# A fused four-layer image kernel: tables made during sampling, the channel norm run backwards with the rows' way back behind it, the columns' way back beside the rows' way ahead, and the next pair's loads issued after the quarter-size convolution

## The chip, the cores and the metric

The kernel runs on one core of a Trainium2 chip, in float32. The metric is the device time of one execution in microseconds (us); lower is better. Five engines work side by side, each through its own instructions in order: PE (matrix products; its weight loads are listed as PEld), DVE (vectors), ACT (activations), POOL (general), and SP, which here only issues DMAs. ACT and POOL can issue DMAs too.

## The reference

The input x has 8 images of 64 channels and 128 x 128 pixels. Four layers follow one another, each adding to x what it makes of a group norm of x (`_gn`, 32 groups of 2 channels):

```python
x = x + L0(_gn(x))   # deformable 3x3 convolution, batch norm over all 8 images, relu
x = x + L1(_gn(x))   # plain 3x3 convolution, 64 to 64 channels
x = x + L2(_gn(x))   # state-space scan along rows and along columns
x = x + L3(_gn(x))   # convolution with stride 4, neighbours, 3x3 convolution, resize by 4
```

L0 makes 18 offsets and 9 masks per pixel with convolutions, samples the image bilinearly at the 9 displaced places and multiplies with the weights. Its batch norm takes mean and variance over all images, so nothing of L1 can start before L0 has ended for every image. L2 does this twice, with the pixels in row order (direction 0) and in column order (direction 1):

```python
fx = layer_norm(seq)                 # over the 64 channels of a pixel
Bu = einsum(fx, B_bar)               # drives 64 complex states
xf = scan(Bu); xb = reversed scan(Bu)
h  = 2 * real(concat(xf, xb) @ C) + D * fx
y  = gelu(h) + fx
y  = layer_norm(y) @ enc.T @ dec.T + layer_norm(y)
```

and fuses both results with a 1x1 convolution. L3 reduces the image to 32 x 32 pixels with a 4 x 4 convolution of stride 4, finds for each pixel the nine least similar ones within a 7 x 7 window, averages their difference, convolves, gates each channel, and enlarges by 4.

## The kernel before

Images are worked on in pairs: partition = image of the pair x channel, so there are four pairs p = 0 to 3. `deform()` does L0 for all pairs, then `rest()` does L1 to L3 pair by pair. The order of the calls in the Python code is the order of priority; a scheduler places each engine's instructions from it with a model of their durations, and an instruction waits by semaphores for its data, for a free buffer of its tag (`bufs`) and, where a pool takes over the addresses of a closed one, for the last reader of those addresses.

**Sampling** (`deform`). Per pair a table of pixels with their neighbours is written to DRAM (`fill`), after `statistics` for the group norm. For 512 pixels at a time, `sample` issues on POOL one indirect DMA for each tap, image and 128 pixels (L379: 9216 in all), DVE multiplies by weights (L388) and sums four corners (L389), PE transposes (L393, L395) and multiplies (L402). A function `work()` is called after every nine gathers, 256 times in a pair; it advances `near` (the offsets of the next 1024 pixels) each time, and `far` (statistics and table of the next pair, 42 steps) every fifth time.

**The setup** (`setup_rest`) follows sampling: the batch norm's scale and bias from `ystat` (L480 to L488), then `setup_scan` (a long chain of small DVE instructions that makes the state tables `tabs` and the output tables `outs` of both directions and stores them in DRAM, L808 and L809), then `setup_nearest` (scales of L3, the mask `window`, the block-diagonal `wa`).

**Per pair.** Two SBUF tiles of the size of an image, `room0` and `room1`, take turns.

- `finish_deform`: x comes in by eight DMAs on SP (L501) and the sampled y by eight on ACT's queue (L503) into a tile with three buffers; ACT applies the batch norm and relu (L504), POOL adds (L505), DVE takes statistics (L507), and `groupnorm` ends it.
- `conv3x3`: L1, PE (L560) and DVE (L562, L566); between its steps it advances `aside`, which is `neighbours` (most of L3) of the pair before.
- `first_norm`: the centred image and its variance per pixel (PE L859 and L824, ACT L861 and L862), then the scale 1/sigma, spread over the channels by POOL (L830) and PE (L833), multiplied in by DVE (L851). It goes through the image in eight steps of 16 rows, n = 0 to 7.
- `scan_direction`, for rows and then for columns, in 16 groups of 1024 pixels. The **way back** goes from the last group to the first: `inputs` (ACT L900, four DMAs on SP L902) puts the pixels in scan order, `drive` (PE L911 and L914, ACT L913, DVE L918, POOL L919) makes the drive u, `scan` (PE L930, ACT L931, DVE L933) the states z, and z is stored to DRAM (L949). The **way ahead** goes from the first group to the last, with `inputs`, `drive` and `scan` again, `rebuilt` (reads z of the way back, L958; PE L962, POOL L966 and L968, DVE L967), `outputs` (PE L981, ACT L983, DVE L984), `deviation` (PE L993 and L997, ACT L995) and `add` (PE L833 and L1012, DVE L1013 and L1017). Before this change the rows' way back starts when `first_norm` has ended, and the columns' way back when the rows' way ahead has.
- `finish_deform` of the next pair, then `down` of this one: its weights `l_wd` (L160, L162), the bias (L1093), scaled weights (L1097), 32 products in two sums (L1103), relu (L1104), store of the small image `kept` (L1107) and of the image to `y` (L1108).

PSUM, where PE writes, has eight banks here: tags "x", "b" and "y" with two buffers each, "small" and "bs" with one. The way back takes "b" and "y" in turn for `drive`; the way ahead takes "b" for `drive` and `rebuilt`.

Of the kernel before, what the change touches and what calls it, by code (L numbers as in the profile page):

```python
# [9 lines left out]
F32 = mybir.dt.float32  # L10
# [6 lines left out]
P = 128  # L17
C = 64
# [22 lines left out]
class Net:  # L41


    def __init__(self, tc, ctx, ins, out):
# [9 lines left out]
        self.ystat = self.const.tile([P, self.npair * NCH, 6], F32, name="ystat")  # L54
# [110 lines left out]


    def deform(self):
# [6 lines left out]
        with ExitStack() as ctx:  # L174
# [242 lines left out]
            for p in range(self.npair):  # L417
                more = p + 1 < self.npair
                far = chain(statistics(p + 1), fill(p + 1)) if more else iter(())
                for e in range(NCH // 2):  # L420
# [6 lines left out]
                    def work(near=near, far=far, count=count):  # L427
                        count[0] += 1
                        next(near, None)
                        if count[0] % 5 == 0:  # L430
                            next(far, None)
# [8 lines left out]
    def rest(self):  # L440
        tc = self.tc
        with ExitStack() as ctx:
            pool = lambda name, bufs, **kw: ctx.enter_context(tc.tile_pool(name=name, bufs=bufs, **kw))
            self.big = pool("b_big", 1)
            self.keep = pool("b_keep", 1)
# [6 lines left out]
            self.state_tab = [self.dram.tile([P, NSTATE], F32, name=f"state_tab{d}") for d in range(2)]  # L452
            self.out_tab = [self.dram.tile([P, NOUT], F32, name=f"out_tab{d}") for d in range(2)]
            self.setup_rest()
# [5 lines left out]
            for p in range(self.npair):  # L460
# [4 lines left out]
                if p + 1 < self.npair:  # L465
                    other = tile_(p + 1, f"room{(p + 1) % 2}")
                    r, nb = self.finish_deform(p + 1, image(other))
                aside = self.neighbours(p, self.down(p, a, r3, nb3))
# [4 lines left out]
    def setup_rest(self):  # L473
        tc, nc, ins, keep = self.tc, self.nc, self.ins, self.keep
        psum = self.ps1

        gamma = self.vec(keep, "gamma", ins["gamma"])
# [12 lines left out]
        self.setup_scan()  # L490
        self.setup_nearest()
# [101 lines left out]
    def setup_scan(self):  # L593
# [12 lines left out]
        with tc.tile_pool(name="b_scan_setup", bufs=1) as sp:  # L606
            pp = self.ps
# [17 lines left out]
            nc.vector.tensor_scalar(phase, phase, -math.pi, math.pi, ALU.max, ALU.min)  # L625
            sin, cos = tl("sin"), tl("cos")
# [65 lines left out]

            for d in range(2):
# [13 lines left out]
                while n < NB:  # L707
# [5 lines left out]
                    n *= 2  # L713

# [13 lines left out]
                for name, gu, gv in (("b", gre, sgim), ("bs", gim, sgre)):  # L728
# [3 lines left out]
                    bm.append(m)  # L732

                mats = tabs[:, MAT : MAT + T * P].rearrange("p (f a q) -> p f a q", f=2, a=2)
                for k in range(T):
# [3 lines left out]
                    tp = pp.tile([P, P], F32, tag="x", name=f"tp{k}_{d}")  # L739
                    nc.tensor.transpose(tp, m, eye)  # L740
                    for f, j in ((0, T - 1 - k), (1, k)):
                        half = slice(j % 2 * C, j % 2 * C + C)
                        nc.vector.tensor_copy(mats[half, f, j // 2], tp[half])

# [22 lines left out]
                for name in ("ln1_g", "ln1_b", "D"):  # L767
                    s[name] = self.vec(keep, f"{name}{d}", ins[name][d])

                for k in range(1 - T, T):  # L770
                    c_ = om[:, 0, k - 1] if k > 0 else om[:, 1, T + k] if k else both_c
                    gp = pp.tile([P, C], F32, tag="x", name=f"gp{k}_{d}")
# [499 lines left out]
```

## Time and profile before

| | us |
|---|---|
| median of 3 runs | 17387.34 (17378.91 to 17398.45) |
| profiled execution, its own time | 17399.76 |
| its span, first to last instruction | 17398.0 |
| mean granted PE clock | 0.826 |

From the trace, where the stages lie (us from the start of the span; pair 2 stands for all):

| stage | from | to |
|---|---|---|
| sampling, all pairs | 224.9 (first gather) | 11951.8 |
| setup | 11951.8 | 12030.5 (first load of x) |
| `finish_deform`, pair 0 | 12030.5 | 12097.7 |
| pair 2: `first_norm` | 14918.6 | 15003.6 |
| pair 2: rows, way back | 15003.6 | 15092.7 |
| pair 2: rows, way ahead (L981) | 15090.1 | 15399.7 |
| pair 2: columns, way back (L949) | 15413.8 | 15493.9 |
| pair 2: columns, way ahead (L981) | 15491.3 | 15802.1 |
| `finish_deform` of pair 3 | 15823.9 | 15893 |
| `down` of pair 2 | 15893 | 15954 |

One execution's trace gives these; a stage is read from the first and last instruction of the lines named. A row of the stage view gives, for a stretch of time, the busy time of each engine in it and its number of instructions, the granted PE clock (1 is full), the share of time in which the 16 DMA engines were busy, and GB/s. Products in float32 are recorded as two PE instructions each. Matmuls are pipelined, so that their busy time is not a measure of PE at its peak.

### The profile page before, as it was taken

What the parts mean: (1) busy time and instruction counts of PE and PEld (TensorE: products, weight loads), DVE (VectorE), ACT (ScalarE), POOL (GpSimd) and SP (SyncE); (2) the same over time, 40 slices, a digit from 0 to 9 for tenths busy, and PEclk for the clock granted to TensorE, in tenths of its full rate; (3) what the DMA queues carried; (4) which work ended last, traced back from release to release, by engine and by line L of the source; (5) the groups of instructions that cost most, each with busy time, mean ns of one, the idle gap of its engine ahead of it and who ended that gap; (6) DMA issues with size and microseconds to landing.
All of it is one profiled execution on the core that took longest, in us unless ns stands there. A gap on an engine that the chain in (4) does not pass through costs nothing. (4 is left out here: it accounts for less than half of the span.)

```text
span 17398.0 us, 124024 instructions
## 1 busy us (share of the span) xinstructions
PE 11757.7 (68%) x33912; PEld 4169.8 (24%) x33912; DVE 11724.9 (67%) x27470; ACT 2920.7 (17%) x4957; POOL 10355.3 (60%) x10489
## 2 busy tenths in 40 slices
PE   5666656656666655666666566533887887887887
PEld 1111111111111111111111111111443443443443
DVE  5777777777777777777777777775564565565565
ACT  1111111011111111111110100001331332332331
POOL 3777777777777777777777777774231232232231
PEclk8877778778877877788878778766998898998998
DMA  6444444444444444444433333333122222222222
GB/s 199 130 138 134 132 136 126 126 129 131 138 134 132 120 131 128 137 135 132 129 116 114 117 114 114 112 107 118 50 64 91 86 64 94 85 65 93 86 63 73
DMA packets 965241, 1968.72 MB, mean 113 GB/s; under 512 B 215740, under 2 KB 516548, under 8 KB 930756
## 3 DMA queue, kind: packets, MB, share of 16 engines
q0 software_dynamic: 442368, 1208.55, 23.7%
q1 hardware_dynamic: 513332, 714.84, 13.4%
q10 hardware_dynamic: 8848, 37.40, 0.6%
q8 instruction: 275, 4.51, 0.1%
q14 instruction: 418, 3.42, 0.1%
HBM read 1515.79 MB, written 276.47 MB: 103 GB/s over the span
## 5 line engine op out<-in xcount | busy, mean ns | idle before, releaser
L379 POOL DMA_INDIRECT g<-table,idx x9216 | 8908.4, 967 | 2811.8 <-issue 2598.9
L388 DVE TENSOR_TENSOR g<-g,wts 128x256 f32<-128x256 f32 x9216 | 3807.8, 419 | 3147.4 <-DMA g<-table,idx 3125.5
L389 DVE TENSOR_REDUCE sm<-g 128x64 f32<-128x256 f32 x9216 | 4978.4, 579 | 0.5
L313 PE MATMUL po<-xe,wt 128*54 128x512 f32 (+3 forms) x8384 | 4780.2, 681 | 54.7 <-ACT ob L323 52.8
L393 PE MATMUL sp<-ident,sm 128*128 128x128 f32 x4096 | 1526.6, 377 | 4108.8 <-DVE sm L389 4099.2
L393 PEld LDWEIGHTS sp<-ident,sm 128*128 128x128 f32 x4096 | 628.4, 155 | 6927.5 <-DVE sm L389 4985.3
L396 ACT COPY s<-sp 128x512 f32<-128x512 f32 x1024 | 600.0, 586 | 8571.9 <-PE sp L393 8571.6
L313 PEld LDWEIGHTS po<-xe,wt 128*54 128x54 f32 x8384 | 931.4, 140 | 1440.4 <-issue 1078.0
L919 POOL TENSOR_TENSOR u<-u,vs 128x512 f32<-128x512 f32 x256 | 347.2, 1356 | 1174.7 <-DVE vs L918 1096.7
L402 PE MATMUL yp<-s,wd 128*64 128x512 f32 (+1 forms) x2560 | 816.1, 654 | 14.3 <-ACT s L396 14.3
L560 PE MATMUL c<-room,l_w 128*64 128x508 f32 (+1 forms) x3072 | 721.5, 597 | 16.7 <-DMA room<-nx 9.2
L900 ACT ACTIVATE fx<-room,ln_b,ln_g 128x512 f32<-128x512 f32 x512 | 646.6, 1292 | 145.9 <-DMA in<-fx 77.5
L911 PE MATMUL pv<-in,tabs 128*128 128x512 f32 x1024 | 560.5, 655 | 61.2 <-DMA in<-fx 58.2
L830 POOL COPY l_yb<-ln_y 128x512 f32<-128x512 f32 x128 | 78.8, 615 | 871.1 <-PE l1v L824 662.5
L395 PE MATMUL s<-ident,sm 128*64 128x128 f32 x1024 | 348.4, 340 | 334.2 <-DVE sm L389 297.2
L981 PE MATMUL py<-in,outs 128*128 128x512 f32 x1024 | 519.0, 611 | 0.0
L981 PE MATMUL py<-x,outs 128*128 128x512 f32 x1024 | 484.1, 594 | 0.0
L933 DVE TENSOR_TENSOR_SCAN z<-tabs,z,u 128x256 f32<-128x256 f32 x512 | 388.8, 778 | 100.6 <-POOL u L919 93.8
L968 POOL TENSOR_TENSOR x<-x,xt 128x512 f32<-128x512 f32 x256 | 324.8, 1269 | 201.8 <-DVE xt L967 201.8
L984 DVE TENSOR_TENSOR h<-h,in 128x512 f32<-128x512 f32 x256 | 285.7, 1118 | 229.8 <-ACT h L983 225.6
L1017 DVE SCALAR_TENSOR_TENSOR room<-room,bias,rs 128x256 f32<-128x256 f32 x512 | 391.4, 823 | 8.9
L397 ACT COPY s<-s 64x128 f32<-64x128 f32 x1024 | 264.1, 258 | 678.1 <-PE s L395 677.7
(1432 smaller groups left out, 10737.0 us busy)
## 6 DMA issues: line engine op xcount, KB each, us to landing
g<-table,idx POOLq DMA_INDIRECT x9216, 2.8
table<-q SPq DMA_DIRECT2D x512, 256.0 KB
in<-fx SPq DMA_DIRECT2D x1024, 128.0 KB
xe<-in_x_dram SPq DMA_DIRECT2D x56, 1408.0 KB
xs<-in_x_dram SPq DMA_DIRECT2D x32, 1024.0 KB
xt<-in_x_dram SPq DMA_DIRECT2D x32, 1024.0 KB
y<-ys SPq DMA_DIRECT2D x128, 256.0 KB
room<-in_x_dram SPq DMA_DIRECT2D x32, 1024.0 KB
```

Source lines behind the costliest of these rows:

```text
L313: nc.tensor.matmul(po[:, r0:r1, c0:c1], lhsT=wt[:, t, :], rhs=xe[:, row + r0 : row + r1, c0 + dx : c1 + dx], start=n == 0, stop=n == len(u ...
L379: nc.gpsimd.indirect_dma_start(out=tq[:, k, :], out_offset=None, in_=flat[i], in_offset=bass.IndirectOffsetOnAxis(ap=idx[:, at : at + 1], ...
L388: nc.vector.tensor_mul(t[:, k], t[:, k], w)
L389: nc.vector.tensor_reduce(sm[:, k], t[:, k].rearrange("p q c -> p c q"), axis=mybir.AxisListType.X, op=ALU.add)
L393: nc.tensor.transpose(sp[:, j, :], sm[:, j * P : (j + 1) * P], self.ident)
L396: nc.scalar.copy(st[i][:, 0:4, m * P : (m + 1) * P], sp)
L402: nc.tensor.matmul(yp[i * C : (i + 1) * C, :], lhsT=wd[0:rows, j, :], rhs=st[i][0:rows, j, :], start=j == 0, stop=j == 4)
L560: nc.tensor.matmul(o, lhsT=lt, rhs=mv, start=k < 2, stop=k >= len(calls) - 2)
L900: nc.scalar.activation(fx[:, e].rearrange("p h (o m) -> p h o m", m=inner), src[:, e::2], AF.Identity, bias=w["ln1_b"], scale=w["ln1_g"])
L911: nc.tensor.matmul(pv, lhsT=tabs[:, at : at + P], rhs=fx[:, :, h, :], start=h == 0, stop=h == 1)
L981: nc.tensor.matmul(py, lhsT=lt, rhs=mv, start=n == 0, stop=n == len(calls) - 1)
L1017: nc.vector.scalar_tensor_tensor(at, at, w["bias"], rs[:, j], ALU.add, ALU.add)
```

## The change

1. **Tables in sampling.** `setup_scan` and `setup_nearest` become generators, 36 steps in all, and are put ahead of `far` of pair 0; they use the PSUM tag "s1" of sampling. `far` is advanced at every third call of `work()` instead of every fifth, in all pairs. Only the batch norm's scale and bias stay after sampling (`setup_deform`). `window` goes to DRAM and is loaded again in `neighbours` of each pair; `wa` is loaded there too.
2. **Norm from the last rows.** `first_norm` runs n = 7 to 0 and yields after each scaled step; after every yield the rows' way back is advanced twice. It takes the tags of the scan's pool for its temporary tiles.
3. **Columns' way back beside rows' way ahead.** `ahead` of direction 0 advances `back` of direction 1 once per group. `drive` uses the PSUM tag "b" everywhere. The tag "in" has two buffers instead of three; the columns' way back has tags of its own with one buffer ("inb", "zbk") and shares "fx", "v" and "u". In `ahead`, `inputs` and `drive` of group g + 2 come ahead of `deviation` of group g.
4. **Loads beside the quarter-size convolution.** `finish_deform` of the next pair is called at the end of `down`, inside its pool, instead of ahead of it.

```diff
+    def run(self):
+        with tc.tile_pool(name="keep", bufs=1) as self.keep:
+            with tc.tile_pool(name="ystat", bufs=1) as sp:
+                self.ystat = sp.tile([P, self.npair * NCH, 6], F32, name="ystat")
+                self.deform()
+                with tc.tile_pool(name="bn0_ps", bufs=1, space=PSUM) as psum:
+                    self.setup_deform(psum)
+            self.rest()
...
                 far = chain(statistics(p + 1), fill(p + 1)) if more else iter(())
+                if p == 0:
+                    far = chain(self.setup(ps_s1, "s1"), far)
...
-                        if count[0] % 5 == 0:
+                        if count[0] % 3 == 0:
                             next(far, None)
...
-            self.setup_rest()
...
-                if p + 1 < self.npair:
-                    other = tile_(p + 1, f"room{(p + 1) % 2}")
-                    r, nb = self.finish_deform(p + 1, image(other))
-                aside = self.neighbours(p, self.down(p, a, r3, nb3))
+                other = tile_(p + 1, f"room{(p + 1) % 2}") if p + 1 < self.npair else None
+                kept, norm = self.down(p, a, r3, nb3, image(other) if other is not None else None)
+                if norm:
+                    r, nb = norm
+                aside = self.neighbours(p, kept)
...
-        for n in range(NCH // 4):
+        for n in range(NCH // 4 - 1, -1, -1):
...
             if late:
                 scale(*late)
+                yield
             late = n, self.rsqrt(self.small, pv, 32, EPS, "ln32")
         scale(*late)
+        yield
...
+            ways = [Scan(self, wp, p, d, a, b, st) for d in range(2)]
+            back = ways[0].back("in", "z", "h")
+            for _ in self.first_norm(wp, p, a, b, r, nb):
+                next(back)
+                next(back)
+            for _ in back:
+                pass
+            ways[0].ahead(ways[1].back("inb", "zbk", "fx"))
+            ways[1].ahead(iter(()))
...
-            out = wp.tile([P, 2, 2, NB], F32, tag="in", name=f"in{p}_{d}{f}_{g}", bufs=3)
+        out = wp.tile([P, 2, 2, NB], F32, tag=itag, name=f"in{name}", bufs=1 if itag == "inb" else 2)
...
+    def back(self, itag, ztag, stage):
+        order = range(NG - 1, -1, -1)
+        fx, u, z = None, None, None
+        for n in range(-2, NG):
+            made = self.drive(1, order[n + 1], fx) if 0 <= n + 1 < NG else None
+            if n + 2 < NG:
+                fx = self.inputs(1, order[n + 2], itag, stage)
+            if n >= 0:
+                z = self.scan(1, order[n], u, z, ztag)
+                self.nc.sync.dma_start(self.net.back[self.d][order[n]], z[:, :, 0:NB])
+            u = made
+            yield
...
+    def ahead(self, aside):
+        self.outs = self.wp.tile([P, NOUT], F32, tag="outs", name=f"outs{self.p}_{self.d}", bufs=1)
+        self.nc.sync.dma_start(self.outs, self.net.out_tab[self.d])
+        fxs, us, xs, late, z = {}, {}, None, None, None
+        for g in range(-2, NG + 1):
+            if 0 <= g + 1 < NG:
+                z = self.scan(0, g + 1, us.pop(g + 1), z, "z")
+            hs = self.outputs(g, fxs.pop(g), xs) if 0 <= g < NG else None
+            if 0 <= g + 1 < NG:
+                xs = self.rebuilt(g + 1, z)
+            if late:
+                self.add(*late)
+            if g + 2 < NG:
+                fxs[g + 2] = self.inputs(0, g + 2, "in", "fx")
+                us[g + 2] = self.drive(0, g + 2, fxs[g + 2])
+            late = (g, hs, self.deviation(g, hs)) if 0 <= g < NG else None
+            next(aside, None)
+        for _ in aside:
+            pass
...
             for n in range(4):
                 s = slice(n * 4096, (n + 1) * 4096)
                 nc.sync.dma_start(self.y[p][:, s], af[:, s])
-        return kept
+            return kept, (self.finish_deform(p + 1, nxt) if nxt is not None else None)
...
+                self.window = wp.tile([P, self.BAND], F32, name=f"window{p}", bufs=1)
+                nc.sync.dma_start(self.window, self.window_tab)
...
+                wa = self.block_diag(sp, f"wa{p}", ins["wa"].rearrange("a (t b) -> a t b", t=1), 1, C)[:, 0, :]
```

## The prediction

> **What bounds the kernel now.** I read the page's 40 slices first, to find its regimes, then the groups of instructions for the longest of them.
>
> ```profile
> PE   5666656656666655666666566533887887887887
> DVE  5777777777777777777777777775564565565565
> POOL 3777777777777777777777777774231232232231
> ...
> L379 POOL DMA_INDIRECT g<-table,idx x9216 | 8908.4, 967 | 2811.8 <-issue 2598.9
> ```
>
> Two regimes: sampling for 27 slices, then four pairs. In sampling the gathers L379 follow one another with 0.30 us between them for which the profile names no other engine ("issue"): 313 start in 400 us while a table is filled (1.278 us each) and 318 where none is (1.258 us). POOL's own issue bounds sampling; DVE has a fifth of its time free. Then the stage view, with stretches cut at the first and last instruction of each stage. Its columns are length, busy time of PE, PEld, DVE, ACT and POOL (instructions in brackets), granted PE clock, DMA share, GB/s.
>
> ```profile
> 11951.70:12030.00 78.30, 18.93 (x56) 13.34 (x56) 64.09 (x383) 2.17 (x4) 2.49 (x12) 0.53 0.15 39
> ```
>
> ```profile
> 14918.00:15003.00 85.00, 77.47 (x450) 55.87 (x450) 42.33 (x155) 40.53 (x64) 19.69 (x32) 0.90 0.00 1
> 15003.00:15093.00 90.00, 60.29 (x137) 24.80 (x138) 46.34 (x69) 56.41 (x68) 22.02 (x16) 0.88 0.57 151
> 15093.00:15384.00 291.00, 265.25 (x1013) 133.31 (x1013) 185.18 (x412) 98.28 (x147) 120.31 (x105) 1.00 0.18 44
> 15384.00:15494.00 110.00, 87.31 (x265) 39.32 (x264) 63.95 (x120) 55.40 (x76) 30.25 (x24) 0.91 0.47 125
> 15494.00:15825.00 331.00, 293.14 (x1141) 147.53 (x1139) 229.99 (x496) 98.46 (x154) 125.28 (x112) 0.98 0.22 65
> 15825.00:15893.00 68.00, 6.32 (x27) 6.01 (x27) 29.72 (x76) 16.75 (x8) 37.62 (x9) 0.50 0.65 251
> 15893.00:15954.00 61.00, 60.77 (x78) 16.83 (x78) 0.22 (x1) 0.97 (x2) 0.17 (x1) 0.93 0.00 0
> ```
>
> The first row is the setup: DVE alone, one small instruction after another. The others are pair 2: norm, rows back, rows ahead, columns back (with edges of its neighbours), columns ahead, the next pair's `finish_deform` (PE empty, DMA at 251 GB/s) and `down` (PE alone). The last two share nothing. Norm and ways ahead, though, are already PE stages, so what is put beside them adds PE work. How much is in the timeline of a way ahead:
>
> ```profile
> 15200.50 0.19 PEld L981 LDWEIGHTS py<-x,outs 128*128 128x128 f32 x1 [0.24 <-issue]
> 15200.93 0.19 PEld L981 LDWEIGHTS py<-x,outs 128*128 128x128 f32 x1 [0.24 <-issue]
> 15201.36 0.19 PEld L981 LDWEIGHTS py<-x,outs 128*128 128x128 f32 x1 [0.24 <-issue]
> ...
> 15204.46 1.08 PE L1012 MATMUL pm<-h,outs 128*64 128x256 f32 x8
> 15207.27 0.66 PE L833 MATMUL 2_0_4_1_rb<-ident,2_0_4_1_yb 128*128 128x128 f32 x4 [1.72 <-POOL 2_0_4_1_yb L830]
> 15207.76 1.02 PE L911 MATMUL pv<-in,tabs 128*128 128x512 f32 x2
> ```
>
> One pass of 512 columns is issued every 0.43 us, and in a group of 20.0 us (POOL's L830 at 15200.59 and 15220.59) PE has one real gap, 1.72 us.
>
> **What the Trainium skill says.** "Perfetto Trace Analysis", section Optimization Strategy, advises interleaving regimes whose most-contended engine differs. The rows above agree for `finish_deform` and `down`, and for setup and sampling; they don't for the ways, where PE leads on both sides. "TensorE: Matmul & The Clock Gate", section Why this matters for your kernels, wants no PE gaps over about 3 us, or the clock drops: clock 0.50 in `finish_deform`, 0.88 on the way back, 1.00 on the way ahead agree. "SBUF — State Buffer", section Who interferes with whom, has DVE copies and tensor-scalar operations in a two-port mode lock GpSimd out; no row here isolates that, so it only bounds a cost below.
>
> **Part 1, tables in sampling.** Removed from the path: 11951.8 to 12030.5. Left is the batch norm's scale and bias, ready at 11962.5 (L488). Relu L504 started at 12045.5, 9.7 us after the first load of y was issued; issued at about 11954 that load lands at 11964, so the pair starts 81 us earlier. I take 78 (65 if addresses come free later, 82 at most). Added to sampling: at most the stage's 383 DVE instructions, 64.1 us, beside 2900 us of pair 0's sampling of which DVE has a fifth free; 12 POOL instructions, 2.5 us, which do hold up gathers; 56 PE passes and a change of ACT's table, both engines waiting there anyway; many small DMAs on SP, where they stand between table stores, not gathers. If each DVE instruction locked POOL out, 64 us; if none, 2.5. I take 8. `far` at every third call does the same fills in 126 calls instead of 210: the 0.020 us that a gather loses to a fill is paid on the same number of stores, so 0 (-40 to +40). Reloading `window` and `wa` is three DMAs a pair under `conv3x3`; only the last pair could show it: 1 us (0 to 4).
>
> **Part 2, norm and rows back.** Now 171.5 us from the first L859 (14918.6) to the rows' first L981 (15090.1). PE busy time is 77.5 + 60.3 = 138. The way back's issue is less: four pv and two pt passes at 0.43 and 0.36 for pn are 2.94 us a group, 47 in sixteen, making 125. DVE (88) and ACT (97) fit below. Not shared are the start (about 8 us until a first step is scaled and read) and the end: after the last scaled step the way back has three steps left at 90/16 = 5.6 us, with PE half idle. I take 155, a gain of 16 a pair (0 if the chains run in series, 35 at PE's sum), 64 in all.
>
> **Part 3, columns back beside rows ahead.** Now 401.2 us from the rows' first L981 (15090.1) to the columns' (15491.3): 15.5 groups of 20.0 us and 91.6 after the last L981 (15399.7). The columns' way ahead still has to wait for the single `outs` buffer, freed by the last L1012 at 15422.3; with a load of some 4 us the 91.6 become 30. So 61.6 us go, and each of 15.5 groups gets x longer: 2.94 us of new PE work less what falls into the gap of 1.72, so at least 1.2. I take x = 2.9, nothing filled, because new chains bring new waits: six uses a group of the two "b" banks instead of four, three "in" buffers become two, one "fx" for two users, and u of the way back must wait for its scan. That is 61.6 - 45 = 16 a pair, 64 in all. Behind a PE instruction that waits for "b" stand L981 and L993, and behind them gelu and DVE. Ends: x = 1.2 gains 43 a pair, x = 5.6 (a whole step of the way back in series) loses 25.
>
> **Part 4, loads beside `down`.** `down` waited for addresses: its memset of `l_wd` came at 13242.8 in pair 0, right behind the last L505, although its norm was ready at 13191.8. Inside the pool it needs none of `finish_deform`'s: weights at about 13192, L1097 till 13197, 58 us of L1103, relu at 13256. `finish_deform` takes its 68 us from 13184 as before, to about 13252, being bound by DMA and POOL, which `down` doesn't use. What is late next is `down`. `conv3x3`, now first active at 13317.7, starts at about 13260: 57 us, three times, 171 (45 to 62 each). Moved queue positions: the loads L501 on SP now follow `kept` (L1107), which waits for the relu, and L503 on ACT follows L1104. But the scheduler already put the stores L1108 at 13184.4 ahead of `kept`, so it doesn't keep call order on SP.
>
> **Sum.** 78 - 8 - 1 + 64 + 64 + 171 = 368 us. The span falls from 17398.0 to 17030; the profiled run has 1.8 us around its span and lay 12.4 above the median, so a median of about 17020.
>
> **Rivals.**
> (a) *Better packing*: waits fall into PE's idle time, x = 1.2 and norm plus rows back 136 us. For it: PE idles 9% of the way ahead, a third of the way back.[...] 78 - 9 + 140 + 172 + 171 = 552, median 16836.
> (b) *PSUM jam*: x = 5.6, and nothing from part 2. For it: "b" alone, where the way back had "b" and "y". Against: each use holds a bank some 3 us of 23. 78 - 9 + 0 - 100 + 171 = 140, median 17248.
> (c) *The loads don't come beside `down`*: L501 or L503 stays queued behind the relu, or addresses still clash. 368 - 171 = 197, median 17190.
> (d) *Sampling slows*: denser fills and DVE's small instructions lengthen gathers. For it: the 0.020 us that a fill costs now, and the port lock. It decides from 368/9216 = 0.040 us a gather; at 0.060 it costs 553, so 17398 - 368 + 553 = 17583 of span, median 17573, 186 slower. Against: gathers never waited for DVE longer than their own issue gap.
>
> **How the numbers follow.** 0.2%, 35 us, is about what a measurement tells from no change. Chances: forecast 0.56, (a) 0.15, (b) 0.12, (c) 0.08, (d) 0.09, of which 0.02 ends within 35 us of before and 0.07 above. So faster 0.91, same 0.02, slower 0.07. The range, 16860 to 17220, takes in the forecast's ends and (c), half of (a) and half of (b).
>
> **What would show it.** In the new profile: no setup stage and a first L501 near 11955; gathers still 313 to 318 in 400 us; `down` and `finish_deform` under each other, 60 us less from the end of a way ahead to L546; rows ahead at about 23 us a group with PE without its gap; 155 us from the norm's first product to L981. A group at 25 us or a gather at 1.31 us would make the forecast wrong.

## Result and profile after

The changed kernel takes 17284.35 us (median of 5 runs, 17278.66 to 17314.63) against 17387.34 us (5 runs): a ratio of 0.9941, 95% interval 0.9925 to 0.9956. That is 103 us less, where 368 were forecast. The profiled execution spans 17276.9 us against 17398.0, 121.1 less.

Cut at the same instructions in both traces, the difference lies here (us, all four pairs together):

| stage | before | after | difference |
|---|---|---|---|
| start to the first activation of `conv3x3` (L546, now L557) | 12097.7 | 12066.6 | -31.1 |
| `conv3x3`, from there to the norm's first product (L859, now L879) | 1007.1 | 1000.4 | -6.7 |
| norm and rows' way back, to the rows' first L981 (now L1208) | 703.1 | 749.6 | +46.5 |
| rows' way ahead, to the columns' first L1208 | 1594.9 | 1592.8 | -2.1 |
| columns' way ahead, `down` and `finish_deform`, to the next L557 (last pair: to its first L975) | 1744.7 | 1619.3 | -125.4 |
| from there to the end | 250.5 | 248.2 | -2.3 |

Parts 1 and 4 paid, less than forecast; part 2 cost time; part 3 did nothing. In the third row one of the four pairs of before is unlike the others: 188.8 us at a granted clock of 0.78, where the other three take 171.3 to 171.6 at 0.88 and 0.89. Against those three the changed kernel's 186.7 to 187.7 us are a loss of some 16 us a pair, more than the sum shows. The 40 slices and the gathers' group of the page after:

```profile
PE   5766565656676656666565665642898898898897
POOL 3777777777777777777777777776132132232231
...
L388 POOL DMA_INDIRECT g<-table,idx x9216 | 8942.7, 970 | 2813.3 <-issue 2617.2
```

The two regimes are still there, and POOL's own issue still bounds sampling (2617.2 us of idle time put to "issue", 2598.9 before). The slices of the pairs have fuller PE digits, and that alone looks like success. The stage view says otherwise. These rows are: what is left between the last gather and the first load of x; pair 2's norm with rows' way back; rows' way ahead; the wait ahead of `down`; `down`.

```profile
11987.50:12001.90 14.40, 7.54 (x20) 2.03 (x20) 6.65 (x7) 1.43 (x3) 0.00 (x0) 0.74 0.20 68
14811.40:14999.00 187.60, 153.59 (x579) 93.70 (x579) 88.22 (x215) 93.06 (x131) 38.73 (x48) 0.79 0.27 69
14999.00:15304.00 305.00, 281.88 (x990) 134.08 (x989) 203.55 (x408) 126.64 (x181) 124.59 (x106) 0.99 0.28 71
...
15732.00:15757.00 25.00, 8.55 (x37) 8.32 (x38) 11.58 (x34) 4.19 (x2) 10.78 (x3) 0.51 1.01 374
15757.00:15822.70 65.70, 58.64 (x71) 14.61 (x71) 19.58 (x47) 14.13 (x9) 29.29 (x10) 0.94 0.38 144
```

The row of the setup has gone. The second row is the surprise. Cut at the same products, the stage before has this row:

```profile
14918.60:15090.10 171.50, 134.43 (x579) 79.00 (x580) 86.11 (x216) 96.16 (x131) 41.11 (x48) 0.89 0.30 79
```

Then 579 PE instructions took 134.4 us; now 579 take 153.6 us, at a granted clock of 0.79 instead of 0.89. Nothing was added and PE got busier: the same products run more slowly. Why, the experiments on part 2 show. The fourth row is what is left unhidden of the loads: 25 us in which the DMA engines are full and PE has little to do.

### The profile page after: what moved, and what is told of

The parts are those of the page before. It is cut to its first block, busy times and chain, and to the rows that moved or that the text cites. A ratio compares the mean times of both kernels' runs of the same rounds, so it can differ in the third digit from the quotient of the medians.

```text
span 17276.9 us, 123578 instructions
## 1 busy us (share of the span) xinstructions
PE 11831.8 (68%) x33912; PEld 4204.3 (24%) x33912; DVE 11804.3 (68%) x27470; ACT 2924.7 (17%) x4956; POOL 10377.4 (60%) x10492
## 3 DMA queue, kind: packets, MB, share of 16 engines
q1 hardware_dynamic: 514532, 715.93, 13.5%
## 5 line engine op out<-in xcount | busy, mean ns | idle before, releaser
L388 POOL DMA_INDIRECT g<-table,idx x9216 | 8942.7, 970 | 2813.3 <-issue 2617.2
L849 POOL COPY l_yb<-ln_y 128x512 f32<-128x512 f32 x128 | 76.6, 615 | 1025.2 <-PE l1v L843 665.9
L1208 PE MATMUL py<-in,outs 128*128 128x512 f32 x1024 | 531.0, 622 | 1.8 <-ACT h L1210 1.8
L1208 PE MATMUL py<-x,outs 128*128 128x512 f32 x1024 | 506.0, 607 | 5.1 <-POOL x L1193 4.9
L1192 DVE TENSOR_TENSOR xt<-zt,tabs 128x512 f32<-128x512 f32 x256 | 175.6, 686 | 266.3 <-POOL x L1193 254.6
```

The lines of the kernel that those rows point to most:

```text
L388: nc.gpsimd.indirect_dma_start(out=tq[:, k, :], out_offset=None, in_=flat[i], in_offset=bass.IndirectOffsetOnAxis(ap=idx[:, at : at + 1], ...
L1208: nc.tensor.matmul(py, lhsT=lt, rhs=mv, start=n == 0, stop=n == len(calls) - 1)
```

## The experiments

Most of these runs fell on chips on which the kernel before takes about 19500 us at a mean granted clock of 0.77, the sampling alone some 2000 us longer; the pairs' stages have the same lengths there, so totals are compared as ratios to the kernel before on the same chip, and stages by their length. The ratio of the changed kernel on such a chip is the first run. The expectations also call PE TensorE, DVE VectorE, ACT ScalarE, POOL GpSimd and SP SyncE.

**after_again**: the changed kernel, unedited.

> The changed kernel itself, unedited, as the base of the comparisons of this call. Its ratio to the kernel before should be 0.992 to 0.998: on the chip of the first result it was 0.994. Where the granted clock is lower, products and not gathers set the end of more of the sampling, so the 31 us won there should shrink, and the ratio lie nearer to 1.

Ratio 0.9917 [0.9900, 0.9934], just under the 0.992 to 0.998 that were expected. The reason given for a ratio nearer to 1 fell, too: PE is busy for 52% of the stretch from 3000 to 9000 us here and for 63% on the first chip, so it isn't the products that set the pace; a gather takes 1053 ns instead of 970, and POOL's idle time ahead of the gathers is 4083.5 us instead of 2813.3. Norm and rows' way back 185.9, 187.7, 202.2 and 187.7 us in the four pairs, rows to columns 395.1 to 399.0: as on the first chip. The third pair's 202.2 comes from the same instructions in the same order: PE is busy 168.0 us there at clock 0.72, 153.9 us at 0.79 in the second. The difference lies at the start. These are the first 36.9 us of the stage in the second pair, then in the third:

```profile
15555.90:15592.80 36.90, 33.80 (x158) 23.34 (x158) 13.57 (x53) 21.94 (x31) 4.73 (x8) 0.82 0.13 29
16839.60:16876.50 36.90, 36.90 (x111) 25.71 (x111) 8.44 (x35) 12.23 (x20) 3.21 (x6) 0.50 0.00 0
```

In the third pair the granted clock stays at 0.50 for all of them, with PE busy throughout, and 111 instructions are done instead of 158. What decides on it wasn't found. The unlike pair of before starts in the same way, with 33.0 us at 0.50.

### Part 2: why the norm became slower

**b_serial**: norm from the last rows as in the change, the calls of rows' way back after it.

```diff
             for _ in self.first_norm(wp, p, a, b, r, nb):
-                next(back)
-                next(back)
+                pass
```

> Only the interleaving of part 2 is undone: the norm still goes from the last rows and uses the scan pool's tags, but the rows' way back starts after it. Theory A (order on ACT): in the changed kernel norm plus rows back takes 187.6 us a pair because the fx activations (L1127) stand ahead of the next squares (L881) on ACT and wait there for the freshly scaled rows, so that PE gets a gap of 4.2 us in each of eight steps and loses clock. In series that gap goes: 85 for the norm and 90 for the way back, about 175, so 12 us less a pair and a total near 17235. Rival B (buffers): the loss comes from what the norm and the way back lost in buffers (one-buffer tags, drive on PSUM tag b alone); then the two stay as slow in series: norm over 95 or way back over 105, 190 to 205 in sum, total 17290 to 17350.

Ratio 0.9887 [0.9859, 0.9914]. The stage takes 154.0, 170.0, 153.0 and 170.1 us, 647 in all, against 703 before and 750 in the changed kernel, and less than either theory had. The calls follow one another here, but the instructions don't: the scheduler starts the way back's first `fx` 26 us after the norm's first product (16792.4 and 16766.3 in pair 2), and PE does products of both chains in turn (first two rows). In the kernel before, the way back's first product comes after the norm's last one, at 15001.74, and a pause of 8.25 us (last row):

```profile
16828.88 1.10 PE L1137 MATMUL pv<-in,tabs 128*128 128x512 f32 x2
16829.82 1.02 PE L879 MATMUL pc<-room,center_r 128*128 128x512 f32 x2
```

```profile
15011.10 4.47 PE L911 MATMUL pv<-in,tabs 128*128 128x512 f32 x6 [8.25 <-DMA in<-fx]
```

So this run too has the two chains side by side, in the scheduler's order. It gains 56 us over before, and putting the calls between the norm's steps costs 103 against it. That the 56 us come from the order of the rows, and not from the other edits of part 2 and `drive` that stay in this run, fits these rows; no run took them apart.

**b_lag**: the way back called one step later.

```diff
-            for _ in self.first_norm(wp, p, a, b, r, nb):
-                next(back)
-                next(back)
+            for n, _ in enumerate(self.first_norm(wp, p, a, b, r, nb)):
+                if n:
+                    next(back)
+                    next(back)
```

> Part 2 stays interleaved, but the rows' way back runs one norm step later: after the first yield it is not advanced, so its fx activations read rows that were scaled a step ago. Theory A (order on ACT): nothing on ACT waits for a scale any more, the gap of PE in each step (4.2 us) goes and the step of 23.7 us falls to 19.5 or less; two more steps of the way back are left at the end (11 us). Norm plus rows back 165 to 172 us instead of 187.6, total near 17220. Rival B (buffers): the steps stay at 23 to 24 us and the end grows, 195 to 200 us, total near 17320.

Ratio 0.9879 [0.9849, 0.9909]; 146.9, 142.9, 140.6 and 157.5 us, 588 in all. That is below both expectations: with the way back a step behind, the interleaving gives more than the prediction wanted of it (155). What happens in a step of the changed kernel shows in ACT's and then PE's timeline (start, duration, operation; in brackets the idle time ahead of it and who ended it):

```profile
14890.37 4.89 ACT L1127 ACTIVATE fx<-room,ln_b,ln_g 128x512 f32<-128x512 f32 x4 [1.19 <-DVE room L871]
...
14895.21 0.67 ACT L881 ACTIVATE sq<-pc,cns 128x512 f32<-128x512 f32 x1
```

```profile
14890.64 1.10 PE L879 MATMUL pc<-room,center_r 128*128 128x512 f32 x2
14895.93 1.21 PE L843 MATMUL l1v<-imgmean,sq 128*128 128x2 f32 x6 [4.19 <-ACT sq L881]
...
14901.73 1.92 PE L879 MATMUL pc<-room,center_r 128*128 128x512 f32 x2
```

ACT waits for the rows that DVE has just scaled (L871), does four `fx` of them in 4.89 us, and only then the square `sq` of a product that PE had ready at 14891.7. PE stands 4.19 us in front of the variances. Afterwards a product of the norm that took 1.10 us before the pause takes 1.92. The Trainium skill, "TensorE: Matmul & The Clock Gate", section Why this matters for your kernels, says that such a pause lowers the clock; the trace agrees, with a pause of 4.19 us and 1.10 going to 1.92. The granted clock itself, in the stretch that ends with the pause and in the 10.3 us behind it:

```profile
14882.60:14896.20 13.60, 9.41 (x49) 5.85 (x47) 10.04 (x23) 7.00 (x9) 3.74 (x4) 1.00 0.27 69
14896.20:14906.50 10.30, 10.30 (x28) 6.52 (x28) 1.24 (x5) 3.98 (x8) 1.17 (x2) 0.50 0.24 63
```

Then it is at 1.00 again until the next step's pause has ended. With the lag, these pauses end, and every one of the norm's products that the stage's timeline lists by itself (26) takes 1.0 or 1.1 us:

```profile
16750.80:16891.40 140.60, 124.96 (x579) 76.95 (x580) 91.00 (x215) 93.34 (x131) 41.91 (x48) 0.97 0.35 92
```

Of the 47 us between this row and the changed kernel's, 153.6 - 125.0 = 28.6 are PE's own busy time. Pause, clock and the order of the calls changed together in this run; the next two try to take them apart.

**b_warm**: eight small products more ahead of each set of variances, to keep PE busy in the pause.

```diff
+                for _ in range(8):
+                    nc.tensor.matmul(pv[:, 8 * m : 8 * m + 2], lhsT=self.ident, rhs=self.imgmean, start=True, stop=True)
                 self.variances(pv, 8 * m, sq)
```

> The changed kernel with eight small products more ahead of every four that take the norm's variances (256 more a pair, overwritten by the real ones; about 30 us of TensorE's time at the full rate), to keep TensorE busy in the gap of each step. Theory M: in this stage the same products take longer where TensorE paused before (two of the norm's products 2.05 us after a pause, 1.10 without; 154 us for 579 products at a granted clock of 0.79 here against 125 us at 0.97 with the way back one step behind); kept busy, the clock rises over 0.85 and the stage stays at 187 us or falls as far as 170, in spite of 256 products more. Rival N: the clock is no cause, the stage is bound by the order of ScalarE and VectorE plus TensorE's own time: it grows by 10 to 30 us, to 197 to 220.

Ratio 1.0158 [1.0143, 1.0174]; the stage takes 290.0 to 293.5 us, over both expectations.

```profile
14979.88:15269.90 290.02, 267.78 (x1091) 201.38 (x1091) 90.00 (x215) 93.62 (x131) 39.74 (x48) 0.65 0.17 45
```

The clock fell to 0.65 though PE was busy for 92% of the stretch, and the stretch began with 88 us at 0.50 in which PE was busy without a break:

```profile
14980.00:15068.00 88.00, 88.00 (x336) 74.36 (x337) 10.46 (x38) 20.03 (x28) 4.78 (x8) 0.50 0.05 12
```

Such a start, shorter, stands in the third pair of after_again without the added products. So products of two columns did not keep the clock up here, but that they held it down isn't shown. The expected 30 us were also too few: eight recorded products of this shape take 0.95 us at clock 1.00 (L843 in the changed kernel), so the 512 recorded ones that were added are some 60 us, an estimate. The run settles nothing about the clock as a cause, and shows that PE's time in this stage is on the path.

**b_fx_d_act**: the order of the calls stays, but `fx` of rows' way back is made on POOL, off ACT's queue. (Its second edit, for part 4, is in another stage and told there.)

```diff
+            if stage == "h":
+                nc.gpsimd.tensor_scalar(to, src[:, e::2], w["ln1_g"], w["ln1_b"], ALU.mult, ALU.add)
+            else:
+                nc.scalar.activation(to, src[:, e::2], AF.Identity, bias=w["ln1_b"], scale=w["ln1_g"])
```

> Two edits of the changed kernel in stages that don't touch. (1) On rows' way back the scaling of the inputs (fx) is done by GpSimd instead of ScalarE; the order of the calls stays. Theory Q: the step of 23.7 us comes from four fx of 4.9 us that wait for the step just scaled and stand in ScalarE's queue ahead of the next squares, on which TensorE waits; off that queue, the step falls below 18 us and norm and rows' way back to 145 to 165 us a pair. Rival R: the wait is for data, whatever the queue (the way back always needs rows just scaled, and TensorE's own order puts its products ahead of the norm's): 185 to 205 us as before. (2) The weights of the quarter-size convolution are loaded on ScalarE's queue, ahead of the next pair's y. Theory S: the loads beside them made them late: they land 4 to 6 us earlier and the end of columns to the next conv3x3 is 3 to 8 us shorter (391 to 394 + a few us in the two stages together becomes 416 to 421 instead of 422 to 425). Rival T: the loads of x and y, delayed behind them, set the end: it stays or grows by up to 5 us.

Ratio 0.9878 [0.9859, 0.9897], for both edits together. The stage takes 161.1, 172.5, 160.9 and 160.8 us: Theory Q, at a clock of 0.89 (0.83 in the second pair). The waits of pair 2's stage (engine, line, who ended the wait, us in total, times, longest), first of the changed kernel over 120 us, then of this run over 110 us:

```profile
PEld l1v L843 <- ACT sq L881: 18.4, 4, 5.0
PE l1v L843 <- ACT sq L881: 15.8, 4, 4.2
```

```profile
ACT sq L881 <- PE pc L879: 41.7, 22, 3.6
...
PEld l1v L843 <- ACT sq L881: 4.3, 7, 0.8
```

PE, with its weight loads, waits no longer than 0.8 us at a time for ACT's squares; ACT waits for PE. This run also takes work from ACT (57.0 us busy instead of 93.1), but b_lag leaves that work where it is (93.3 us) and ends the pauses too, by its order alone; and here the way back still needs the rows just scaled. So the queue order on ACT is the cause of the loss. How much of the loss is the lower clock and how much the pauses themselves stays open.

### Part 3: where its gain went

**c_serial**: columns' way back after rows' way ahead, all else as changed.

```diff
-            ways[0].ahead(ways[1].back("inb", "zbk", "fx"))
+            ways[0].ahead(iter(()))
+            for _ in ways[1].back("in", "z", "h"):
+                pass
```

> Only part 3's interleaving is undone: the columns' way back runs after the rows' way ahead, with the rows' tags; two in buffers and drive on tag b stay. Theory C (PE is full): rows ahead goes from 23.2 us a group back to 20.0 to 20.6, the columns' way back costs its 90 us again; from the rows' first L1208 to the columns' 400 to 415 us against 398.9, so total 17285 to 17350. Rival D (part 3 is worth the 16 us a pair that were forecast, and something else in the way back hides it): 415 or more, total 17350 or more.

Ratio 0.9987 [0.9970, 1.0004]; rows to columns 422.1 to 423.1 us, as Rival D had it, against 395.8 to 401.2 before in the same serial order. Interleaving is worth 24 us a pair, but something else in the change costs about as much. Two groups of rows follow each other in 20.55 us here, by the copies L849 that open them:

```profile
17314.56 0.94 POOL L849 COPY 2_0_5_0_yb<-ln_y 128x512 f32<-128x512 f32 x1 [0.79 <-DVE ln_y L118]
17335.11 0.94 POOL L849 COPY 2_0_6_0_yb<-ln_y 128x512 f32<-128x512 f32 x1 [0.79 <-DVE ln_y L118]
```

**c_serial_in3**: the same with three buffers of the tag "in", as before the change.

```diff
-        ... name=f"in{name}", bufs=1 if itag == "inb" else 2)
+        ... name=f"in{name}", bufs=1 if itag == "inb" else 3)
```

> Columns' way back after rows' way ahead, with three buffers of the tile in instead of two. Against the run of the same order with two buffers (rows' way ahead 20.6 us per group, rows to columns 422 us, columns to the next convolution 363 us), Theory I says that the third buffer is what the kernel before had more: 19.9 to 20.1 us per group, rows to columns 400 to 412 us, columns 350 to 355 us, total some 30 us per pair, 120 us, lower than with two. Rival J: the order of the calls in the loop (the deviation after the next inputs) makes the 0.6 us, not the buffer: 20.5 to 20.7 us per group as before, and no gain over 20 us in all.

```profile
17205.32 1.03 POOL L849 COPY 2_0_5_0_yb<-ln_y 128x512 f32<-128x512 f32 x1 [5.08 <-DVE ln_y L118]
17225.32 1.04 POOL L849 COPY 2_0_6_0_yb<-ln_y 128x512 f32<-128x512 f32 x1 [5.11 <-DVE ln_y L118]
```

20.00 us a group, as before the change: the third buffer makes the 0.55 us, and POOL idles 5.1 us ahead of the copy instead of 0.8. From the rows' first L1208 to the columns' last group 737.7 us in pair 2, against 752.6 with two buffers and 724.8 before: 15 of the 28 us. Ratio 0.9936 [0.9920, 0.9951]. Theory I held for the group; rows to columns, at 412.8 to 415.8, fell by 6 to 10 and not to 400 to 412. The other 13 us, all in the passage from rows to columns (120.0 instead of 105.9), weren't found.

**c_early**: the first two steps of columns' way back taken ahead of rows' way ahead.

```diff
+            side = ways[1].back("inb", "zbk", "fx")
+            next(side)
+            next(side)
-            ways[0].ahead(ways[1].back("inb", "zbk", "fx"))
+            ways[0].ahead(side)
```

> The first two steps of columns' way back (two inputs and one drive) are taken before rows' way ahead begins. Theory K: the slow first groups of rows (95 us for two and a half, 23.2 us each later) come from filling both chains at once with one buffer for in, fx and z on the way back: rows to columns falls from 399 to 375 to 390 us, 40 to 90 us in all. Rival L: the slowness is that of products and the VectorE's queue, whoever fills: rows to columns stays within 395 to 402 us, or moves to the end of rows' way back, and the total stays within 20 us of the changed kernel.

Ratio 0.9938 [0.9921, 0.9954]; rows to columns 397.0 to 397.4 us, and norm with rows' way back 201.5 to 204.3, some 15 us later. Theory K fell, and the time moved to the end of rows' way back, as Rival L said; the total, at 19376.85 us against 19344.60, is 32 us longer, where Rival L had at most 20, but the two intervals overlap. The expectation had also misread the first products: their intervals are whole groups at first and halves later. By the copies L849 the first groups are slower all the same, but less (23.9, 31.6 and 25.9 us in the changed kernel).

**c_mid**: columns' step called ahead of `add` instead of last in the loop.

```diff
+            next(aside, None)
             if late:
                 self.add(*late)
...
-            next(aside, None)
```

> In rows' way ahead the step of columns' way back is called after the group's rebuilt states and ahead of the adding, instead of last in the loop. If the place of its calls is what makes a group 23.2 us and the first three slow, rows to columns moves by more than 10 us from 399, in either direction; if the sum of the products and VectorE's work of both sets it, it stays within 395 to 403.

Ratio 1.0066 [1.0051, 1.0081]; rows to columns 435 to 447 us, groups of 25 to 27.5 us instead of 23.2 after a first one of 42.1, for the same instructions. Norm and rows' way back, which the edit doesn't touch, also takes some 10 us a pair more (195.8 to 211.1). The place of the calls in the loop is worth more than the whole of part 3, and the change had the better one of these two.

### Parts 1 and 4 undone

**a_undone**: the tables made after sampling again (`setup` called behind `setup_deform` instead of in `far`).

> Part 1 undone alone: the tables are made after the sampling again, in a stage of their own, all else as in the changed kernel. Theory G: making the tables in the sampling costs the sampling most of what the missing stage gains (the last gather begins some 40 us earlier again), so the undoing costs 25 to 45 us (ratio to the changed kernel 1.0015 to 1.0026). Rival H: the sampling's 37 us are not from the tables but from the run or from the fills; then the stage of some 75 us comes back whole and the undoing costs 65 to 85 us (ratio 1.0038 to 1.0049), with the last gather where it was.

Ratio 0.9928 [0.9912, 0.9944], not told apart from the changed kernel's; the medians, 19383.24 and 19344.60 us, are 39 us apart, which would be Theory G's. The traces of one execution each speak for Rival H: from the last gather to the first activation of `conv3x3` 149.0 us instead of 81.3, so the stage comes back nearly whole, and from the first gather to the last 13780.2 against 13783.6, so the tables cost sampling 3 us. Executions of one kernel lie up to 60 us apart here, and sampling takes 2000 us longer on this chip, so what the tables cost on the first one stays open.

**d_undone**: `finish_deform` ahead of `down` again.

```diff
-                other = tile_(p + 1, f"room{(p + 1) % 2}") if p + 1 < self.npair else None
-                kept, norm = self.down(p, a, r3, nb3, image(other) if other is not None else None)
-                if norm:
-                    r, nb = norm
+                other = None
+                if p + 1 < self.npair:
+                    other = tile_(p + 1, f"room{(p + 1) % 2}")
+                    r, nb = self.finish_deform(p + 1, image(other))
+                kept, norm = self.down(p, a, r3, nb3, None)
```

> Only part 4 is undone: finish_deform of the next pair is called ahead of down again, outside its pool. Theory E: from the end of a columns' way ahead to the next conv3x3's first activation 133 us again instead of 90.7, three times, so 127 us more: total near 17410. Rival F (the overlap is an illusion, since conv3x3 waits for something else too, or finish_deform runs faster without down beside it): under 80 us more, total under 17365.

Ratio 1.0019 [1.0006, 1.0032], 0.010 above the changed kernel. From the columns' last group (its L849) to the next L557 it takes 142.0 to 142.2 us, as before, against 99.2 to 99.4: part 4 is worth 43 us a pair, three times, 128. The ratio is further apart than that, about 200 us: in the profiled execution sampling also ended 35 us later (last gather at 14051.0 instead of 14016.3), and the two ratios come from two chips. Theory E held.

Most of the 14 us missing a pair are in front of `down`. SP's queue, then PE's and DVE's, in the changed kernel:

```profile
15732.06 0.33 SPq L980 DMA_DIRECT2D y<-room  x1
15734.15 4.80 SPq L161 DMA_DIRECT2D l_wd<-in_l_wd_dram  x2
15739.00 7.96 SPq L980 DMA_DIRECT2D y<-room  x3
```

```profile
15747.78 6.96 PE L965 MATMUL pb<-gn_nb,l_wd 128*128 128x1 f32 x32 [11.44 <-DMA l_wd<-in_l_wd_dram]
15756.58 1.25 PE L975 MATMUL pd<-room,l_wr 128*128 128x512 f32 x1 [1.84 <-DVE l_wr L969]
```

```profile
15753.47 1.88 DVE L518 BATCH_NORM_STATS2 gn_st<-room 128x6 f32<-128x512 f32 x3 [2.00 <-POOL room L516]
15755.26 1.27 DVE L969 TENSOR_SCALAR l_wr<-l_wd,gn_y 128x2048 f32<-128x2048 f32 x1
```

`l_wd` is issued at 15734.15 and lands at 15747.7, 13.5 us later, beside the stores of the image and the next pair's loads; L969 then stands behind statistics of the next pair on DVE until 15755.26. At the other end `groupnorm`'s product L125 of the next pair, whose statistics are ready at 15805.8, stands behind L975 on PE till 15814.35, and the next `conv3x3` behind it till 15822.70.

The second edit of **b_fx_d_act** loads `l_wd` on ACT's queue. Without it between them, SP issued all four stores first, and `l_wd` came behind a load of y on its own queue:

```profile
17714.54 11.36 SPq L980 DMA_DIRECT2D y<-room  x4
```

```profile
17714.74 0.32 ACTq L514 DMA_DIRECT2D yr<-y  x1
17716.63 2.42 ACTq L161 DMA_DIRECT2D l_wd<-in_l_wd_dram  x2
```

It landed 24.7 us after its issue, and from the columns' last group to L557 it took 127.1 us instead of 99.4, of which 9.5 came back in `conv3x3`. Theory S has the cure wrong; that the loads beside the weights make them late is shown below, in edit (3) of best. The Trainium skill, "DMA: Bandwidth & Descriptors", section Queues, rings and completion order, says that each DMA engine serves the queues of SP and ACT in turn. No run here shows that by itself; the trace shows that another queue did not bring the weights in sooner, 24.7 us against 13.5, with a load of y ahead of them on that queue.

### Two versions that are faster

**best**: three edits, one in each of three stages: the lag of b_lag, and these two.

```diff
-                fxs[g + 2] = self.inputs(0, g + 2, "in", "fx")
+                third = self.d and (g + 2) % 3 == 0
+                fxs[g + 2] = self.inputs(0, g + 2, "inb" if third else "in", "fx")
...
-                nc.scalar.dma_start(y, self.y[p][:, s])
+                nc.sync.dma_start(y, self.y[p][:, s])
```

> Three edits in three stages that don't touch each other, each read from its own stage. (1) Rows' way back one step behind the norm, as in the run b_lag: norm and rows' way back 140 to 158 us a pair instead of 187 to 202. (2) On columns' way ahead every third input takes the tile inb, free by then, so that the ring is of three: Theory I has the columns' groups at 20.0 instead of 20.6 us and the first inputs of columns loaded earlier, rows to columns 385 to 395 us instead of 399, columns to convolution 345 to 352 instead of 356 to 359; a rival, that the groups are bound by their order of calls, leaves all of it. (3) The y loads of the next pair go out on SyncE's queue, behind the weights of the quarter-size convolution: if the weights' late landing (13 us) was due to the y loads beside them, end of columns to the next pair's first conv3x3 is 5 to 8 us shorter; if the loads of x and y bound it, it stays or grows by up to 10. Sum 200 to 280 us below the changed kernel, ratio to the kernel before 0.976 to 0.982 on this chip.

17066.77 us, ratio 0.9816 [0.9802, 0.9829], on a chip as fast as the first. (1) 144.5 to 145.5 us, as expected. (2) Columns' groups 20.0 us, first to last 292.6 instead of 303.4; rows to columns didn't move (397.0 to 402.8). (3) `l_wd`, in the same place among SP's stores but with no loads of y on ACT's queue beside it, landed 7.6 us after its issue instead of 13.5, and `down`'s products began 25.6 us after the last group began instead of 33.3, but the next pair's loads then ended later: 123.7 us from the last group to L557 instead of 99.4, of which 9 came back in `conv3x3`. The edit loses.

**best2**: (1) and (2) without (3).

> The edits (1) and (2) of the run best without (3): rows' way back one step behind the norm, and a third input buffer for columns; the y loads stay on ScalarE's queue. Read by stages it should give norm and rows' way back 145 us a pair, rows to columns 399, columns to convolution 343 to 350, convolution to the next conv3x3 66 again instead of 98, and conv3x3 272 again instead of 263. The loss of (3) was then 13 to 15 us a pair, and the total is 30 to 50 us below best, ratio to the kernel before 0.977 to 0.980. A rival: the shorter conv3x3 and columns' end of best came from (2) and not from (3); then the total is up to 100 us below best.

Ratio 0.9796 [0.9779, 0.9813], on a chip of the slower sort, where the changed kernel has 0.9917: the fastest version by ratio, though the intervals of best and best2 overlap. Norm and rows' way back 159.1, 145.0, 144.3 and 145.1 us; columns' groups 20.0; last group to L557 99.5 to 99.6. A pair's stages sum to 1229 us against 1243 in best, so the loss of (3) was 14 us a pair, and its rival fell.

## Why the prediction was wrong

| term | forecast, us | measured, us | how |
|---|---|---|---|
| part 1, stage gone | +78 | +77.1 | last gather to L557: 157.2, now 80.1 |
| part 1, sampling | -8 | -46 in the profile | first gather 9.0 later; from first to last 11752.6, before 11715.6 |
| part 2 | +64 | -46.5 | sums of four pairs |
| part 3 | +64 | +2 | rows' first L1208 to columns' last group, pair 2: 724.8, now 724.3 |
| part 4 | +171 | +128 | 142.0 to 142.4 a pair, now 99.2 to 99.4 |

These rows are read from one execution of each kernel, whose spans are 121 us apart. Part 2 is the largest part of what is missing (110 us), then part 3 (62), part 4 (43) and sampling (38).

- **Part 1** was right in its mechanism and in the gain of the stage; the term for sampling was too small. Nothing was set aside for the 9 us by which the first gather starts later, and the 8 us for the tables and 0 for the fills became 37, 16 of them in pair 0, in whose sampling the tables are made. Three other runs of the same sampling on a chip of that speed (best, c_mid, b_warm) took 11723 to 11733 us from the first gather to the last, 20 to 29 less than this execution and 8 to 18 more than before; whether the rest is this chip's or this execution's isn't shown. Rival (d) didn't happen at its size, 0.040 us a gather: 37 us are 0.004. While a table is filled, 307 to 313 gathers start in 400 us (1.28 to 1.30 us each), mostly under the 313 to 318 of the forecast, but for a shorter time.
- **Part 2** has the wrong sign. The step of the prediction that failed is "DVE (88) and ACT (97) fit below": the sums fit, the order doesn't. ACT does its queue in order, and `fx` of a step waits for that step's last scaling, so it holds up the squares that feed PE; the sum of busy times can't show that. The second mistake was to count PE's 125 us as fixed. The prediction quoted the clock's rule and then didn't apply it to the pauses that the new waits would make: the same 579 instructions took 153.6 us.
- **Part 3** had the group right: 23.2 us (forecast 22.9), and PE idles 8% of rows' way ahead (281.9 us busy of 305.0), about as before, so its gap wasn't filled, as the term assumed. Which of the new waits keeps it open wasn't isolated; c_mid shows that the order of the calls counts. The passage shrank from 105.9 to 34.8 us, by 71 (forecast 61.6). Against that the rows' groups, first to last, grew from 296.5 to 353.4, by 57 and not 45, as the first of them are slower (the second took 31.6 us). The step that failed is the sum: it counted the two "in" buffers as a risk for rows and left out that columns run with them too, 293.2 to 303.4 us, -10. The start of rows took 3 us more.
- **Part 4** had the right mechanism and was too large by 14 us a pair. The steps that were mis-sized: weights "at about 13192", some 8 us after the columns' end, came at 16; the scaled weights then queued on DVE; and behind `down` the next norm's product waited for PE.
- Of the rivals, (b) had the number nearest to the result (17248) for a wrong reason: rows' groups took 23.2 and not 25.6 us, no run shows the banks "b" as the cause of anything, and part 2 lost time by ACT's queue.

## What to carry to other kernels

When two chains are interleaved, write down for each in-order queue which instruction of the second chain stands in front of which of the first, and whether its data is a step old; one step of lag turned a loss of 47 us in four pairs into a gain of 115. Sums of busy time are a floor only while PE stays busy: here a pause of 4.2 us was followed by 10.3 us at half the granted clock. Read from the trace, too, whether calls that stand in series run in series: in b_serial they didn't. A buffer that is taken to make an overlap possible has to be paid for in every loop that uses its ring, also in those that don't overlap.

## What was not expected of the hardware

- The same stage of the same program has two lengths, 187.7 and 202.2 us, 153.0 and 170.0, 160.9 and 172.5, by the granted clock of the pair (0.79 and 0.72, 0.92 and 0.83, 0.89 and 0.83), without anything different in its instructions. In the longer 202.2 us the clock stays at 0.50 for the first 36.9 us, with PE busy all that time; in the kernel before, one pair of four is like that.
- With many products of two columns added, PE was busy for 92% of a stretch and the granted clock was 0.65; its first 88 us were at 0.50 with PE busy without a break.
